# A selective-scan layer on one core: input products made two units ahead in three buffers, state sums taken every two units

## The chip, the core and the metric

The program runs on one core of a Trainium2 chip. The metric is the device time of one execution in microseconds (us); a kernel's time is the median of several executions. The engines are named as in the profile: PE multiplies matrices, PEld loads its weights, DVE is the vector engine, ACT the scalar engine, POOL the general one (GpSimd), SP issues most transfers. Each engine takes its instructions in the order in which the program lists them, and waits at one whose inputs or buffers aren't ready.

## What is computed

Four sequences of 512 steps and 512 channels pass through three residual blocks, each after a layer norm. The change touches the first block, a selective scan over 1024 inner channels with 16 states each:

```python
def step(h, inputs):
    d_t, B_t, C_t, u_t = inputs
    dA = jnp.exp(d_t[..., None] * A)
    h = h * dA + (d_t * u_t)[..., None] * B_t[:, None, :]
    y = jnp.einsum('bdn,bn->bd', h, C_t)
    return (h, y)
...
y = jnp.swapaxes(ys, 0, 1) + u * D
y = y * jax.nn.silu(jnp.transpose(z, (0, 2, 1)))
```

Here `u` is a convolved and gated projection of the input, and `d_t` a softplus of another one. The second block is a pair of linear layers with quantized operands. The third is a mixture of 16 experts, two for each token, with one shared expert.

## The kernel before

**Units of the scan.** The scan goes through the four sequences (batches, b = 0 to 3) one after another, and through each in eight chunks c of 128 channels. A chunk has eight units n; a unit holds 64 channels and 4 of the 16 states, as a tile of 128 partitions by 2 x 512 steps. `UNITS` gives for each n the state group g and the half p of the chunk's channels: p = 0 for n = 0, 1, 4, 5 and p = 1 for n = 2, 3, 6, 7. There are 4 x 8 x 8 = 256 units, here numbered 0 to 255. One turn of the loop in `scan_batch` is called a slot, and slot n scans unit n.

**What a unit costs.** Two exponentials on ACT write the decays `da` (L663; two buffers, in PSUM). One product on POOL writes the inputs `bu` = B x (step x u) (L665; two buffers). On DVE the scan runs over `da` and `bu` and writes into `da` (L672), and a product with C writes `h` (L678; five buffers). PE sums `h` over states into one accumulator `py` (L690), after a product that adds u x D (L686). When all eight units are summed, DVE gates the result into `u` (`gated`, L712).

**When they are issued.** Slot n issues `unit_inputs` of unit n + 1 (decays and product), later the scan of unit n and its product with C. The sums come twice for each chunk: those of units 0 to 3 at slot 4, those of units 4 to 7 at slot 0 of the next chunk, and the gating at slot 1.

**What the products read.** `delta` computes the steps of a chunk: PE (L610), six passes on ACT (L622 to L632), and four on POOL (L634 to L640) with a small fill (L642) that ends them. `spread` then copies the result, with SP, into `rep` (L650; three buffers, one for each half-chunk, 2 x 512 KB), in which each row stands four times. B and C come in `bc` tiles (L601), loaded anew for each batch by `scan_bc`.

**Work beside the scan.** While the scan runs, the kernel computes the inputs of later batches (`front`: projections on PE, ACT's convolution taps L447 and L452, POOL's additions L456) and finishes earlier ones (`back`: output projection, quantized layers, routing; `experts`: tiles of 128 tokens, each with two gathers issued by POOL, L1419 and L1175). These are generators that yield what they wait for. `Pace` estimates, while the program is built, how far each engine has got. `more` is called three times in a slot and issues the next step of each generator if `Pace.clear` allows it: no engine of the step may be more than `BEHIND` (ns) behind the estimate of DVE's time, and what the step waits for must be ready at most `SLACK` (ns) after it; engines other than DVE get an allowance of 3500, 1200 or 0 ns on top, by the place in the slot. For POOL they are 500 and -300. Where steps of a chunk are late for their copy, `end` issues them at once. So the order of instructions on each engine is fixed when the program is built.

After the last scan, the rest of batch 3 (output projection, quantized layers, routing) and the remaining expert tiles run; two gathers for each 128 tokens and DVE's L1223 write the output.

Of the kernel before, what the change touches and what calls it, by code (L numbers as in the profile page):

```python
# [19 lines left out]
P = 128  # L20
# [112 lines left out]
class Pace:  # L133
# [6 lines left out]
    TABLES = {"Exp": 0, "Tanh": 0, "Silu": 1, "Ln": 2}  # L140


    SLACK = {"DVE": 200, "Activation": 700, "Pool": -300, "PE": 3500, "SP": 500}
    BEHIND = {"DVE": 0, "Activation": 1500, "Pool": 500, "PE": 5000, "SP": 4000}

    def __init__(self, nc):
        self.nc, self.seen, self.table, self.queue = nc, 0, None, 0
# [122 lines left out]
class Kernel:  # L270
# [225 lines left out]
    def first_front(self, sb, bank):  # L496

        nc, st = self.nc, self.state[0]
        xnT = self.xnT0
        for j in range(4):  # L500
            self.load_win(0, sb, j)
        for _ in self.layernormed(0, sb, bank, xnT):
            pass
        nc.sync.dma_start(self.wx_sb, self.wx)
        nc.sync.dma_start(self.wdt_sb, self.wdt)
        pj = {}
        pdt = bank.take([P, L])
        pbc = bank.take([P, L])


        pairs = [(b, self.fsideT[b], 0, k) for b in range(B) for k in (0, 2)]
        pairs += [(b, self.ctxwT[b], NK, 0) for b in range(B)]
        each = -(-len(pairs) // NC)
        held = {}

        def columns(c):
            for i in range(c * each, min((c + 1) * each, len(pairs))):
                b, w, _, k = pairs[i]
                held[i] = self.sb.tile([P, NP, L], F32, name="h", bufs=5)
# [36 lines left out]
        st["dt"] = self.sb.tile([P, L], F32, name="dt", bufs=1)  # L556
        nc.scalar.copy(st["dt"], pdt)
        bank.done(pdt)
        rows = sb.tile([2 * DS, L], F32, name="rows", bufs=1)
        nc.scalar.copy(rows, pbc[: 2 * DS])  # L560
        bank.done(pbc)
        nc.sync.dma_start(self.rows_d[0], rows)
        self.done.add(("rows", 0))
        for g in range(NG):
            self.scan_bc(0, g)
# [86 lines left out]
            )  # L652
        st["rep"][c, p] = rep

    def unit_inputs(self, b, c, n):

        nc, st = self.nc, self.state[b]
        g, p = UNITS[n]
        rep = st["rep"][c, p]
        da = self.pscan.tile([P, NP, L], F32, name="da", bufs=2)  # L660
        for i in range(NP):
            q = c * NQC + p * NP + i
            nc.scalar.activation(da[:, i, :], rep[:, i, 0, :], AF.Exp, scale=self.a_sb[:, q, g : g + 1])  # L663
        bu = self.sb.tile([P, NP, L], F32, name="bu", bufs=2)
        nc.gpsimd.tensor_mul(bu, st["bc"][0, g].unsqueeze(1).to_broadcast([P, NP, L]), rep[:, :, 1, :])  # L665
        st["da"][c, n], st["bu"][c, n] = da, bu

    def unit_scan(self, b, c, n):
        st = self.state[b]
# [4 lines left out]
    def unit_out(self, b, c, n):  # L674
        st = self.state[b]
        g, p = UNITS[n]
        h = self.sb.tile([P, NP, L], F32, name="h", bufs=5)
        self.nc.vector.tensor_mul(h, st["da"].pop((c, n)), st["bc"][1, g].unsqueeze(1).to_broadcast([P, NP, L]))  # L678
        st["h"][c, g, p] = h

    def state_sums(self, b, c, g0):

        nc, st = self.nc, self.state[b]
        if g0 == 0:
            st["py"] = self.pscan.tile([P, L], F32, name="py", bufs=1)
            nc.tensor.matmul(st["py"], self.skips.pop((b, c)), st["u"][c], start=True, stop=False)  # L686
        py = st["py"]
        for g in range(g0, g0 + 2):
            for q in range(NQC):
                nc.tensor.matmul(  # L690
                    py[q * CH : (q + 1) * CH, :],
                    self.sel,
                    st["h"][c, g, q // NP][:, q % NP, :],
                    start=False,
                    stop=(g == NG - 1),
                )

    def skip(self, b, c):
# [798 lines left out]
    def run(self, ctx):  # L1497
# [21 lines left out]
        with tc.tile_pool(name="front", bufs=2) as fsb:  # L1519
# [16 lines left out]
            self.unit_inputs(0, 0, 0)  # L1536
# [61 lines left out]
    def finish(self, b, n):  # L1598

        if n == 0:  # L1600
            self.state_sums(b, NC - 1, NG // 2)
        elif n == 1:
            self.gated(b, NC - 1)

    def scan_batch(self, b, beside):

        self.started.add(b)
        for i in range(NC * NU):
# [3 lines left out]

            nb, nc = following(b, c, (n + 1) // NU)
            if nb < B:
                self.unit_inputs(nb, nc, (n + 1) % NU)

            if n == 4:
                self.state_sums(b, c, 0)
            if n == 0 and c:
                self.state_sums(b, c - 1, NG // 2)  # L1620
            if b and not c:
                self.finish(b - 1, n)
            self.more(beside, 3500)
# [5 lines left out]
            if n == 2:  # L1629
                self.gate(b, c)  # L1630
                self.steps_of(*following(b, c, 2))

            if n == 5:
                self.skip(*following(b, c, 2))
                self.copies.append((*following(b, c, 1), 1))
            if n == 7:
                self.copies.append((*following(b, c, 2), 0))
            while self.copies:
                db, dc, p = self.copies[0]
                if db < B:  # L1640
# [78 lines left out]
```

## Time and profile before

| what | us |
|---|---|
| median of three runs (1672.4 to 1674.71) | 1673.51 |
| the profiled execution | 1669.61 |
| its span | 1667.9 |
| first scan starts | 89.7 |
| last scan ends | 1343.9 |
| DVE busy from first to last scan, 1254.2 us | 1076.2 |
| POOL busy in the same | 974.5 |
| PE busy in the same | 926.4 |
| ACT busy in the same | 779.1 |

The profile is one execution. A group line names the source line, engine, operation, tiles (written <- read) and count, then the busy time and the mean of one in ns, then the idle time of the engine just before such instructions and what ended most of it. A line of the waits names who waited for whom, the total in us, the number of times and the longest. A line of the timeline has the start, the duration, the instruction, and in brackets the idle time before it and what ended it. [...]

### The profile page before, as it was taken

How to read it: one execution, taken by the hardware profiler on the slowest of the kernel's cores; microseconds unless marked ns; L12 is line 12 of the kernel's file. 1: busy time of each engine (PE TensorE's matmuls, PEld its weight loads, DVE VectorE, ACT ScalarE, POOL GpSimd, SP SyncE). 2: the span in 40 equal slices, each digit the busy share in tenths (PEclk: the TensorE clock that was granted, in tenths of full speed). 3: DMA queues.
4: the chain of work that ended last, by engine and by line, in shares of the span. 5: the costliest groups of instructions: out<-in, count | busy, mean ns of one | idle time of the engine just before them, and what ended most of it. 6: DMA issues, size and time to landing. Idle time of an engine off the chain costs nothing. (4 is left out here: it accounts for less than half of the span.)

```text
span 1667.9 us, 15571 instructions
## 1 busy us (share of the span) xinstructions
PE 1216.4 (73%) x4552; PEld 585.6 (35%) x4552; DVE 1220.5 (73%) x1322; ACT 895.6 (54%) x1448; POOL 1125.6 (67%) x904
## 2 busy tenths in 40 slices
PE   6867588649676759799776985875656897668980
PEld 2222122103242323233433432363434346434760
DVE  4377899998898896789887998988777933453312
ACT  2365677654668764654886652478654313530330
POOL 1176999887788894777887874878887544027454
PEclk9988789768787978799988897987797999768995
DMA  5564464565463463675443758535577472158957
GB/s 204 150 160 111 98 148 95 125 150 148 106 123 67 110 167 107 152 194 155 91 106 88 194 126 292 139 105 146 146 212 207 123 299 105 52 204 295 360 207 221
DMA packets 109657, 262.21 MB, mean 157 GB/s; under 512 B 16192, under 2 KB 20416, under 8 KB 109504
## 3 DMA queue, kind: packets, MB, share of 16 engines
q1 hardware_dynamic: 93120, 204.50, 46.7%
q0 software_dynamic: 16448, 56.65, 9.8%
q8 instruction: 40, 0.66, 0.2%
q14 instruction: 49, 0.40, 0.1%
HBM read 168.55 MB, written 45.88 MB: 129 GB/s over the span
## 5 line engine op out<-in xcount | busy, mean ns | idle before, releaser
L665 POOL TENSOR_TENSOR bu<-bc,rep 128x1024 f32<-128x1024 f32 x256 | 602.0, 2357 | 171.2 <-DVE da L672 130.5
L672 DVE TENSOR_TENSOR_SCAN da<-da,bu 128x1024 f32<-128x1024 f32 x256 | 585.8, 2288 | 81.2 <-POOL bu L665 60.3
L663 ACT ACTIVATE da<-rep,a_sb 128x512 f32<-128x512 f32 x512 | 352.9, 691 | 298.8 <-DVE h L678 261.5
L678 DVE TENSOR_TENSOR h<-da,bc 128x1024 f32<-128x1024 f32 x256 | 312.0, 1219 | 15.6 <-PE py L690 5.1
L690 PE MATMUL py<-h,sel 128*32 128x512 f32 x1024 | 172.2, 673 | 68.5 <-DVE h L678 68.4
L1175 POOL DMA_INDIRECT wx<-in_wexp,wrow x62 | 62.9, 1015 | 92.6 <-PE bank L1465 29.0
L400 PE MATMUL bank_a<-xnT,win 128*128 128x512 f32 x176 | 91.2, 666 | 12.9 <-DVE gz L357 8.3
L456 POOL TENSOR_TENSOR u<-u,tap 128x511 f32<-128x511 f32 (+2 forms) x72 | 91.2, 1266 | 9.2 <-ACT tap L452 6.7
L690 PEld LDWEIGHTS py<-h,sel 128*32 128x32 f32 x1024 | 30.6, 116 | 187.3 <-DVE h L678 109.9
L400 PE MATMUL bank_g<-xnT,win 128*128 128x512 f32 x176 | 90.0, 659 | 4.4 <-DVE gz L357 2.1
L1419 POOL DMA_INDIRECT xs<-xn_d,tok x62 | 64.0, 1032 | 19.7 <-issue 15.2
L400 PE MATMUL bank_b<-xnT,win 128*128 128x512 f32 x128 | 64.0, 646 | 17.1 <-ACT sp_r L623 17.1
L400 PEld LDWEIGHTS bank_a<-xnT,win 128*128 128x128 f32 x176 | 36.5, 215 | 62.8 <-issue 48.1
L634 POOL TENSOR_TENSOR sp_e<-sp_e,dd 128x512 f32<-128x512 f32 x32 | 40.6, 1270 | 26.2 <-ACT dd L629 26.0
L400 PEld LDWEIGHTS bank_g<-xnT,win 128*128 128x128 f32 x176 | 36.3, 214 | 59.3 <-issue 48.8
L335 POOL TENSOR_SCALAR ln_scale<-ln_mv 128x1 f32<-128x1 f32 x48 | 11.0, 229 | 61.6 <-DVE ln_mv L328 58.5
L686 PE MATMUL py<-u,skip 128*128 128x512 f32 x64 | 37.5, 671 | 13.5 <-DVE u L712 13.5
L1213 POOL DMA_INDIRECT yg<-y_d,pos x32 | 32.5, 1014 | 21.3 <-DMA y_d<-ys 9.3
L400 PEld LDWEIGHTS bank_b<-xnT,win 128*128 128x128 f32 x128 | 26.4, 212 | 52.9 <-issue 29.4
L1223 DVE SCALAR_TENSOR_TENSOR xr<-yg,topw,xr 128x512 f32<-128x512 f32 x32 | 23.8, 751 | 28.4 <-DMA yg<-y_d,pos 27.8
L640 POOL TENSOR_TENSOR dd<-dd,u 128x512 f32<-128x512 f32 x32 | 40.6, 1269 | 1.5
L636 POOL TENSOR_TENSOR sp_e<-sp_e,sp_r 128x512 f32<-128x512 f32 x32 | 40.6, 1268 | 1.4
(404 smaller groups left out, 2386.4 us busy)
## 6 DMA issues: line engine op xcount, KB each, us to landing
rep<-dd SPq DMA_DIRECT2D x128, 512.0 KB
win<-in_win SPq DMA_DIRECT2D x64, 256.0 KB
x<-xr SPq DMA_DIRECT2D x48, 256.0 KB
xr<-x SPq DMA_DIRECT2D x48, 256.0 KB
y_d<-ys SPq DMA_DIRECT2D x48, 256.0 KB
bc<-rows_d SPq DMA_DIRECT2D x32, 256.0 KB
gz_d<-gz SPq DMA_DIRECT2D x32, 256.0 KB
gzl<-gz_d SPq DMA_DIRECT2D x32, 256.0 KB
```

The lines of the kernel that those rows point to most:

```text
L400: nc.tensor.matmul(pj, win[:, k, :], xnT[:, k, :], start=(k == 0), stop=(k == NK - 1))
L456: nc.gpsimd.tensor_add(u[:, j:], u[:, j:], v[j][:, j:])
L634: nc.gpsimd.tensor_sub(e, e, du)
L636: nc.gpsimd.tensor_add(e, e, r)
L640: nc.gpsimd.tensor_mul(du, delta, st["u"][c])
L663: nc.scalar.activation(da[:, i, :], rep[:, i, 0, :], AF.Exp, scale=self.a_sb[:, q, g : g + 1])
L665: nc.gpsimd.tensor_mul(bu, st["bc"][0, g].unsqueeze(1).to_broadcast([P, NP, L]), rep[:, :, 1, :])
L672: self.nc.vector.tensor_tensor_scan(daf, daf, buf, 0.0, ALU.mult, ALU.add)
L678: self.nc.vector.tensor_mul(h, st["da"].pop((c, n)), st["bc"][1, g].unsqueeze(1).to_broadcast([P, NP, L]))
L690: nc.tensor.matmul(py[q * CH : (q + 1) * CH, :], self.sel, st["h"][c, g, q // NP][:, q % NP, :], start=False, stop=(g == NG - 1),)
L1175: nc.gpsimd.indirect_dma_start(out=ws[s], out_offset=None, in_=self.wexp, in_offset=bass.IndirectOffsetOnAxis(ap=wrow[:, s : s + 1], axis= ...
L1419: nc.gpsimd.indirect_dma_start(out=xs[s], out_offset=None, in_=xn_d, in_offset=bass.IndirectOffsetOnAxis(ap=tok[:, s : s + 1], axis=0), bo ...
```

## The change

`unit_inputs` is split. The decays stay one unit ahead. The products are issued two units ahead, into three buffers, at the same place of the slot; the first two are issued before the loop. `h` gives up one of its five buffers for the third `bu`. The state sums are taken for each two units: units n - 2 and n - 1 at slot 2, 4 and 6, the last two at slot 0 of the next chunk. The copies of the steps are queued and forced one slot earlier, the second half's at slot 4, the next chunk's first half at slot 6. B and C of the next batch, first half, are loaded at slot 3, not 4. `Pace` lets POOL be 3500 ns behind, not 500, and lets its steps wait 2500 ns, not -300.

```diff
-    SLACK = {"DVE": 200, "Activation": 700, "Pool": -300, "PE": 3500, "SP": 500}
-    BEHIND = {"DVE": 0, "Activation": 1500, "Pool": 500, "PE": 5000, "SP": 4000}
+    SLACK = {"DVE": 200, "Activation": 700, "Pool": 2500, "PE": 3500, "SP": 500}
+    BEHIND = {"DVE": 0, "Activation": 1500, "Pool": 3500, "PE": 5000, "SP": 4000}
...
-        bu = self.sb.tile([P, NP, L], F32, name="bu", bufs=2)
-        nc.gpsimd.tensor_mul(bu, st["bc"][0, g].unsqueeze(1).to_broadcast([P, NP, L]), rep[:, :, 1, :])
-        st["da"][c, n], st["bu"][c, n] = da, bu
+        st["da"][c, n] = da
+
+    def unit_products(self, b, c, n):
...
+        bu = self.sb.tile([P, NP, L], F32, name="bu", bufs=3)
+        nc.gpsimd.tensor_mul(
+            bu, st["bc"][0, g].unsqueeze(1).to_broadcast([P, NP, L]), st["rep"][c, p][:, :, 1, :]
+        )
+        st["bu"][c, n] = bu
...
-        h = self.sb.tile([P, NP, L], F32, name="h", bufs=5)
+        h = self.sb.tile([P, NP, L], F32, name="h", bufs=4)
...
-        for g in range(g0, g0 + 2):
-            for q in range(NQC):
+        for g, p in UNITS[2 * i : 2 * i + 2]:
+            h = st["h"].pop((c, g, p))
+            for j in range(NP):
+                q = p * NP + j
...
             nb, nc = following(b, c, (n + 1) // NU)
             if nb < B:
-                self.unit_inputs(nb, nc, (n + 1) % NU)
-
-            if n == 4:
-                self.state_sums(b, c, 0)
+                self.unit_decays(nb, nc, (n + 1) % NU)
+            nb, nc = following(b, c, (n + 2) // NU)
+            if nb < B:
+                self.unit_products(nb, nc, (n + 2) % NU)
+
+            if n and n % 2 == 0:
+                self.state_sums(b, c, n // 2 - 1)
             if n == 0 and c:
-                self.state_sums(b, c - 1, NG // 2)
+                self.state_sums(b, c - 1, NU // 2 - 1)
...
+            if n == 4:
+                self.copies.append((*following(b, c, 1), 1))
             if n == 5:
                 self.skip(*following(b, c, 2))
-                self.copies.append((*following(b, c, 1), 1))
-            if n == 7:
+            if n == 6:
                 self.copies.append((*following(b, c, 2), 0))
...
-                    late = (db, dc) == following(b, c, 1) and n == NU - 2 + p or (db, dc) == (b, c)
+                    late = (db, dc) == following(b, c, 1) and n == NU - 3 + p or (db, dc) == (b, c)
...
-            if b + 1 < B and c == NC - 1 and n in (4, 7):
+            if b + 1 < B and c == NC - 1 and n in (3, 7):
```

More of the change, by code (lines that the diff above doesn't have):

```diff
@@ L518, in columns @@
                 b, w, _, k = pairs[i]
-                held[i] = self.sb.tile([P, NP, L], F32, name="h", bufs=5)
+                held[i] = self.sb.tile([P, NP, L], F32, name="h", bufs=4)
                 nc.sync.dma_start(held[i], w[k * P : (k + 2) * P, :].rearrange("(k p) n -> p k n", k=2))
@@ L653, in spread, with unit_decays @@
         st["rep"][c, p] = rep
-    def unit_inputs(self, b, c, n):
+    def unit_decays(self, b, c, n):
         nc, st = self.nc, self.state[b]
@@ L663, in unit_inputs @@
             nc.scalar.activation(da[:, i, :], rep[:, i, 0, :], AF.Exp, scale=self.a_sb[:, q, g : g + 1])
-        bu = self.sb.tile([P, NP, L], F32, name="bu", bufs=2)
-        nc.gpsimd.tensor_mul(bu, st["bc"][0, g].unsqueeze(1).to_broadcast([P, NP, L]), rep[:, :, 1, :])
-        st["da"][c, n], st["bu"][c, n] = da, bu
+        st["da"][c, n] = da
+    def unit_products(self, b, c, n):
+        nc, st = self.nc, self.state[b]
+        g, p = UNITS[n]
+        bu = self.sb.tile([P, NP, L], F32, name="bu", bufs=3)
[3 more added lines that the diff above has]
+        st["bu"][c, n] = bu
     def unit_scan(self, b, c, n):
@@ L676, in unit_out, with state_sums @@
         g, p = UNITS[n]
-        h = self.sb.tile([P, NP, L], F32, name="h", bufs=5)
+        h = self.sb.tile([P, NP, L], F32, name="h", bufs=4)
         self.nc.vector.tensor_mul(h, st["da"].pop((c, n)), st["bc"][1, g].unsqueeze(1).to_broadcast([P, NP, L]))
         st["h"][c, g, p] = h
-    def state_sums(self, b, c, g0):
+    def state_sums(self, b, c, i):
         nc, st = self.nc, self.state[b]
-        if g0 == 0:
+        if i == 0:
             st["py"] = self.pscan.tile([P, L], F32, name="py", bufs=1)
@@ L687, in state_sums @@
         py = st["py"]
-        for g in range(g0, g0 + 2):
-            for q in range(NQC):
+        for g, p in UNITS[2 * i : 2 * i + 2]:
+            h = st["h"].pop((c, g, p))
+            for j in range(NP):
+                q = p * NP + j
                 nc.tensor.matmul(
[L691 to L695, printed above, removed]
+                    py[q * CH : (q + 1) * CH, :], self.sel, h[:, j, :], start=False, stop=(g == NG - 1)
                 )
@@ L1535, in run @@
             self.fronts = Steps(self.pace, (w for b in range(1, B) for w in self.front(b)))
-            self.unit_inputs(0, 0, 0)
+            self.unit_decays(0, 0, 0)
+            for n in range(2):
+                self.unit_products(0, 0, n)
             pool = ctx.enter_context(ExitStack())
@@ L1600, in finish @@
         if n == 0:
-            self.state_sums(b, NC - 1, NG // 2)
+            self.state_sums(b, NC - 1, NU // 2 - 1)
         elif n == 1:
```

## The prediction

> **What bounds the kernel now.** I read the busy time by stages first, cut at the first scan's start and the last scan's end. Columns: busy time and count of PE, PEld, DVE, ACT, POOL, then the granted clock and the share of the transfer engines.
>
> ```profile
> 89.70:1343.90 1254.20, 926.43 (x3280) 409.46 (x3281) 1076.22 (x1007) 779.09 (x1225) 974.48 (x718) 0.85 0.55 139
> 1343.90:1667.90 324.00, 230.72 (x1141) 153.27 (x1139) 108.78 (x269) 86.35 (x181) 137.75 (x156) 0.84 0.63 222
> ```
>
> The chain of waits that ended last covers only the final 36 us, so the stages decide. The scan stage is three quarters of the span, and DVE is its fullest engine, 1076.2 of 1254.2 us. Nothing shortens that work, so the change can win at most DVE's idle time there, 178 us. POOL has 974.5, 86% to 78%. Next, the groups of a unit on the page:
>
> ```profile
> L665 POOL TENSOR_TENSOR bu<-bc,rep 128x1024 f32<-128x1024 f32 x256 | 602.0, 2357 | 171.2 <-DVE da L672 130.5
> L672 DVE TENSOR_TENSOR_SCAN da<-da,bu 128x1024 f32<-128x1024 f32 x256 | 585.8, 2288 | 81.2 <-POOL bu L665 60.3
> L663 ACT ACTIVATE da<-rep,a_sb 128x512 f32<-128x512 f32 x512 | 352.9, 691 | 298.8 <-DVE h L678 261.5
> L678 DVE TENSOR_TENSOR h<-da,bc 128x1024 f32<-128x1024 f32 x256 | 312.0, 1219 | 15.6 <-PE py L690 5.1
> ```
>
> A unit is 2.288 + 1.219 = 3.51 us of DVE. POOL needs 2.357 for its product, and waits 130.5 us for scans to give back a `bu` buffer while DVE waits 60.3 us for products: two engines that stop each other in turn. What DVE waited for in the stage (window from 89 us on):
>
> ```profile
> DVE da L672 <- POOL bu L665: 60.3, 22, 27.4
> DVE da L672 <- ACT da L663: 20.6, 17, 5.7
> DVE u L712 <- PE py L690: 15.8, 5, 7.6
> ...
> DVE h L678 <- PE py L690: 5.1, 3, 2.6
> ```
>
> The longest, 27.42 us, stands before the first scan. That leaves 21 waits for products in the stage, 60.3 - 27.42 = 32.9 us. DVE's timeline shows three long ones, 8.58 (at 169.77), 4.10 (1251.61) and 5.17 us (1267.99), together 17.85; the other 18 lie between 0.15 and 1.67 us and make 15.0. A short one, POOL's lines and then DVE's:
>
> ```profile
> 203.32 1.26 POOL L638 TENSOR_TENSOR dd<-sp_e,sp_w 128x512 f32<-128x512 f32 x1
> 204.55 2.35 POOL L665 TENSOR_TENSOR bu<-bc,rep 128x1024 f32<-128x1024 f32 x1
> ```
>
> ```profile
> 206.93 2.30 DVE L672 TENSOR_TENSOR_SCAN da<-da,bu 128x1024 f32<-128x1024 f32 x1 [1.24 <-POOL bu L665]
> ```
>
> Two steps of 1.26 us (L636, L638) stood in POOL's queue ahead of a product that DVE needed at once. The long one at 169.77:
>
> ```profile
> 156.90 1.27 POOL L640 TENSOR_TENSOR dd<-dd,u 128x512 f32<-128x512 f32 x1
> 158.24 0.10 POOL L642 MEMSET dd<- 128x1 f32 x1
> 167.39 4.66 POOL L665 TENSOR_TENSOR bu<-bc,rep 128x1024 f32<-128x1024 f32 x2 [9.06 <-DMA rep<-dd]
> ```
>
> Here the steps of chunk (0, 2) were ready only at 158.3, and their copy took 9.06 us; that at 1267.99 is the same at chunk (3, 6) (6.69 us of POOL's idle time before it).
>
> **Products two ahead.** In slot n the product goes out at the same place as before, and it waits for the same event: before, product n + 1 with two buffers, now product n + 2 with three, both for scan n - 1. So POOL gets no more work and no later start; each product is only due a unit later, 3.51 us at least. Against this, `Pace` lets POOL's other steps run 3.0 us further behind (500 to 3500), so up to 3.0 of the 3.51 can be filled with queued steps, and behind a step that waits stand the products, for which DVE waits.
> - Short waits, 15.0 us. At best all go. If the planner fills all it may, each loses 0.51 us: five are 0.49 or less, 1.48 together, and 13 lose 0.51, 8.1 in all. In the built order the largest heaps of other steps between two products are hardly larger than before, so I take 12.
> - Long waits, 17.85. Each can lose 3.51: 3 x 3.51 = 10.5. They lose nothing if the copy is what comes last; the decays need it too, and stay one ahead. In the built order the end of the steps (L642) stands at the same product as before in both chunks, so one slot earlier. I take 6.
> - What is late next is the decays: 0.691 x 2 = 1.4 us of ACT after the last read of their buffer, beside a scan of 2.29, so 0.9 us to spare. In nearly all the short waits longer than 0.3 us the decays had ended 1.8 us or more before DVE came free: at 206.93 ACT's pair ended at 203.52, and DVE at 205.69. Some waits will pass to them: I set 4 us against the gain (bounds 0 and 10; their waits are 20.6 now).
>
> **State sums by two units.** The same 512 matrix products. Sixteen records took 1.92 us at 533.96; after a chunk's last `h` half as many are left before gating, 0.96 us less in each of the five waits of L712 (15.8 us) and in the one after the last scan (3.12): 5 us. An `h` buffer is now asked back four units after it was written, its sums issued two slots earlier, about 9 us (2 x 3.51 + 2.29) ahead of need, where it was 5.8 (3.51 + 2.29): the 5.1 us of L678 should go. Against it PE now stops for an `h` four times a chunk, not twice; it stopped 109.9 + 68.4 us (PEld and PE, overlapping) without being the fullest engine, but what stands behind it on PE (projections for ACT and POOL) starts later. Between +10 and -5 I take 6.
>
> **Copies and loads a slot earlier.** The same 128 copies and 32 loads of B and C on SP's queue, with their 512 and 256 KB, in nearly the same order; SP's wait for the last reader of `rep` (38.7 us for ACT, 13.9 for POOL) is off DVE's path. I count nothing. If a copy is late after all, it costs what the row at 167.39 shows, up to 9 us a time. The second half of B and C isn't loaded earlier, though needed a slot earlier; no wait for `bc` stands in the trace, so nothing.
>
> **After the last scan.** In the built order 48 expert tiles are left, not 46. From 1549.94 to 1628.84 the second group's 23 weight gathers go out, 3.6 us a tile, so two tiles cost 7 us uncovered. They are of the first group and lie ahead of batch 3's routing, which is bound by its chain of layers: from 1400 to 1480 PE is busy 54.6 of 80 us. But from 1344 to 1380 PE is busy 35.7 of 36 us. Bounds 0 and 7; I take 2.
>
> **A rule that speaks against it.** All products ran 2336 to 2697 ns, median 2355, beside scans of 2264 to 2299: neither shows that it had to wait for the other. The Trainium skill, "SBUF — State Buffer", "Who interferes with whom", says that a DVE instruction with two SBUF inputs and a GpSimd one that reads SBUF exclude each other. Scan and product with C each read one operand from PSUM, and the trace agrees. If the rule caught them, a unit would be 2.29 + 1.22 + 2.36 = 5.9 us, and lead would be worth nothing; units took 4.9 us on average, background work included.
>
> **The sum.** 12 + 6 - 4 + 6 - 2 = 18 us. The profiled execution took 1669.61 (span 1667.9 and 1.7 around it), 3.9 below the median of 1673.51; I take the same difference off the median: 1655.5.
>
> **Rivals.**
> - The lead is spent by the planner, and the decays take over the waits: 8 from the short waits, nothing from the long, 2 from PE, less 2 and 2: -6, 1667.5. For it: the thresholds return 3.0 of 3.51 us. Against it: a queue that is filled only at times still gains.
> - The stage gains and the end gives it back: 7 us for the tiles, and PE's stops taking the 5 that they may, 18 - 5 - 11 = 2: 1671.5, no change. For it: PE and transfers (0.94) are full at 1344 to 1380. Against it: the slack until 1480.
> - Slower: POOL waits at the head of its queue. Its steps may now be queued 2.5 us before their inputs are ready, where 0.3 us after was asked, 2.8 in all. In the first batch POOL is already nearly as full as DVE (230.2 and 241.2 of 270.4 us; 96.9 of 100 from 200 to 300), so a wait of 2.8 us in each of its eight chunks, 22 us, is paid there. With half of the gains left (12 of 18 with the rest): 1673.5 + 22 - 12 = 1683.5. It decides from the point at which such waits in a slot exceed the 3.51 us of lead. For it: the steps wait for ACT now already (L634 for L629 16.1 us in 7). Against it: in the built order the other steps stand in nearly the same slots.
>
> **How the numbers follow.** Forecast 0.52, planner 0.18, end 0.10, slower 0.20. The range goes from all bounds on the good side, 15 + 10.5 + 10 = 35.5 less, 1638, to the slow rival, 1684. About 0.2%, 3.3 us, is what a measurement can tell from no change: faster 0.68 (forecast, and nearly all of the planner's case), same 0.12, slower 0.20.
>
> **What would show it.** Right: DVE's waits for products in the stage fall from 32.9 to some 15 us, three long ones among them; POOL's wait for scans stays near 130; the waits of L712 and L678 for PE fall by half; DVE's busy time in the stage stays at 1076. Wrong: waits for the decays well above 25 us, POOL's waits at L634 or L456 for ACT doubled, or an end longer than 331 us after the last scan. My range fails if batch 3's tiles or the order of the quantized layers move so that DVE waits for PE or POOL in new places, which the counts can't tell.

## The result, and the profile after

| | kernel before | changed kernel |
|---|---|---|
| median of 20 runs each, us | 1670.90 | 1673.28 |
| the profiled execution, us (its span) | 1669.61 (1667.9) | 1679.47 (1677.7) |
| first scan to last scan, us | 1254.2 | 1265.8 |
| after the last scan, us | 324.0 | 320.4 |

The ratio of the times is 1.0009, 95% interval 0.9996 to 1.0022: no change that can be told. (A ratio here is taken over all runs and can differ by some 0.001 from that of the two medians.) The forecast was 1655.5. The profiled execution of the changed kernel is 6 us above its median; what only its length shows is not used below.

The groups of the changed kernel that answer to those shown of before, with one more, the sums on PE:

```profile
L671 POOL TENSOR_TENSOR bu<-bc,rep 128x1024 f32<-128x1024 f32 x256 | 601.4, 2360 | 172.9 <-DVE da L680 117.7
L680 DVE TENSOR_TENSOR_SCAN da<-da,bu 128x1024 f32<-128x1024 f32 x256 | 585.8, 2288 | 81.5 <-POOL bu L671 48.0
L663 ACT ACTIVATE da<-rep,a_sb 128x512 f32<-128x512 f32 x512 | 352.9, 691 | 253.2 <-DVE h L686 221.2
L700 PE MATMUL py<-h,sel 128*32 128x512 f32 x1024 | 279.0, 676 | 82.1 <-DVE h L686 81.9
L686 DVE TENSOR_TENSOR h<-da,bc 128x1024 f32<-128x1024 f32 x256 | 312.0, 1219 | 12.8 <-PE py L700 1.8
```

Its waits of DVE over the whole span (who waited for whom, total in us, times, longest):

```profile
DVE da L680 <- POOL bu L671: 48.0, 7, 27.2
DVE da L680 <- ACT da L663: 31.5, 23, 5.2
...
DVE xn L1081 <- PE bank_a L1058: 16.3, 4, 9.7
...
DVE xr L1096 <- PE bank_g L1090: 10.8, 5, 2.7
...
DVE u L718 <- PE py L700: 9.8, 6, 3.6
```

The stage and the rest (us, busy us of PE, PEld, DVE, ACT, POOL, with instructions, then PE's granted clock, the transfers' share, GB/s):

```profile
91.50:1357.30 1265.80, 1002.82 (x3270) 411.84 (x3270) 1073.62 (x1005) 775.00 (x1222) 971.01 (x712) 0.88 0.55 137
1357.30:1677.70 320.40, 230.15 (x1150) 155.25 (x1150) 108.86 (x271) 86.87 (x184) 143.13 (x163) 0.84 0.64 228
```

Three things are to be seen. What the change aims at came: without the wait of 27.2 before the first scan, DVE waits 20.8 us for products in the stage, 32.9 before, and less for the sums. Other waits grew: decays from 20.6 to 31.5, and DVE in front of the shared expert's results (L1081 16.6 and L1096 21.2 us in the stage; the same lines took 6.3 and 7.5 before). And DVE's own work in the stage is the same (1073.6 and 1076.2), while PE is busy 76 us longer there (1002.8 and 926.4). A second profile of the same instructions (s2 below, span 1667.1 us) has the same two waits: 20.9 us for products, 30.6 for decays.

### The profile page after: what moved, and what is told of

Its sections match the earlier page's. It is cut to its first block, busy times and chain, and to the rows that moved or that the text cites. A ratio compares the mean times of both kernels' runs of the same rounds, so it can differ in the third digit from the quotient of the medians.

```text
span 1677.7 us, 15580 instructions
## 1 busy us (share of the span) xinstructions
PE 1294.1 (77%) x4552; PEld 590.7 (35%) x4552; DVE 1218.2 (73%) x1322; ACT 892.2 (53%) x1448; POOL 1127.5 (67%) x904
## 5 line engine op out<-in xcount | busy, mean ns | idle before, releaser
L671 POOL TENSOR_TENSOR bu<-bc,rep 128x1024 f32<-128x1024 f32 x256 | 601.4, 2360 | 172.9 <-DVE da L680 117.7
L700 PE MATMUL py<-h,sel 128*32 128x512 f32 x1024 | 279.0, 676 | 82.1 <-DVE h L686 81.9
L700 PEld LDWEIGHTS py<-h,sel 128*32 128x32 f32 x1024 | 47.7, 116 | 264.0 <-DVE h L686 134.0
L1181 POOL DMA_INDIRECT wx<-in_wexp,wrow x62 | 63.0, 1016 | 93.4 <-PE bank_g L1471 24.7
L456 POOL TENSOR_TENSOR u<-u,tap 128x511 f32<-128x511 f32 (+2 forms) x72 | 91.2, 1267 | 38.0 <-ACT tap L452 35.7
L400 PE MATMUL bank_g<-xnT,win 128*128 128x512 f32 x216 | 109.3, 653 | 0.8 <-ACT xnT L386 0.7
L400 PE MATMUL bank_a<-xnT,win 128*128 128x512 f32 x144 | 69.8, 630 | 2.2 <-DVE gz L357 1.2
L400 PEld LDWEIGHTS bank_g<-xnT,win 128*128 128x128 f32 x216 | 43.4, 209 | 62.2 <-issue 56.0
L694 PE MATMUL py<-u,skip 128*128 128x512 f32 x64 | 37.1, 664 | 24.7 <-DVE u L718 24.7
L357 DVE SCALAR_TENSOR_TENSOR hs<-hs,bank 128x128 f32<-128x128 f32 x24 | 6.9, 286 | 53.3 <-ACT hs L1462 40.7
L341 ACT ACTIVATE xn<-xr,ln_scale 128x512 f32<-128x512 f32 x32 | 25.6, 808 | 37.2 <-POOL ln_scale L337 37.2
L1456 PE MATMUL bank<-xT,wx 128*128 128x128 f32 x368 | 44.3, 277 | 0.0
```

The lines of the kernel that those rows point to most:

```text
L400: nc.tensor.matmul(pj, win[:, k, :], xnT[:, k, :], start=(k == 0), stop=(k == NK - 1))
L456: nc.gpsimd.tensor_add(u[:, j:], u[:, j:], v[j][:, j:])
L700: nc.tensor.matmul(py[q * CH : (q + 1) * CH, :], self.sel, h[:, j, :], start=False, stop=(g == NG - 1))
L1181: nc.gpsimd.indirect_dma_start(out=ws[s], out_offset=None, in_=self.wexp, in_offset=bass.IndirectOffsetOnAxis(ap=wrow[:, s : s + 1], axis= ...
L1456: nc.tensor.matmul(ph[:, i, :], w[:, o : o + P], xT[:, k, :], start=(k == 0), stop=(k == NK - 1))
```

## The experiments

**Theories.** (1) The lead is worth 12 to 25 us, and another placement of background steps, above all near the last scans, gives it back. (2) The lead gains nothing. (3) The sums for each two units cost what the lead gains. Two more came up later: (4) a placement of background steps fits only the loop that it was planned for, and loop and placement have no price apart; (5) the sums hold PE longer.

Loop and placement move together, since the planner (`Pace`) places the steps of each loop anew. To part them, its choices were written down for one kernel (the steps that each call of `more` issues, the slot of each copy, the choice of expert tiles) and replayed in another. The core of that edit, here with P for the recorded choices:

```diff
-            x.go_if_clear(x.due(self.slot) if x.due else 0)
+            at = 2 * self.turn + (x.name in seen)
+            seen.add(x.name)
+            if not x.over and x.written < P["steps"][x.name].get(at, 0):
+                x.go()
```

"Old placement" is that of the kernel before, "new placement" that of the changed kernel. All replayed kernels but e4, e12 and e14 have the changed kernel's copies and loads of B and C, s1 too; on the old placement three of the 62 copies came one unit earlier by that than recorded. That a replay costs nothing by itself is seen in e12, where the old loop, but for the order of its sums, runs on its own recorded placement: 0.9997. Each time is a ratio to the kernel before on the same chip, since chips differ (the kernel before took 1657 to 1673 us).

| loop | placement | ratio (95% interval) |
|---|---|---|
| before | old (its own) | 1 |
| + sums by two (e4) | old | 1.0177 (1.0146 to 1.0209) |
| + sums by two, four h (e9) | old | 1.0184 (1.0154 to 1.0214) |
| + sums by two, four h, lead (e1) | old | 1.0172 (1.0144 to 1.0201) |
| + lead, four h, sums by four (e3) | old | 1.0261 (1.0233 to 1.0289) |
| before, with the copies and loads of the change (s1) | new | 1.0063 (1.0041 to 1.0085) |
| + sums by two, four h (e2) | new | 1.0052 (1.0033 to 1.0071) |
| + sums by two, four h, lead: the changed kernel | new (its own) | 1.0009 (0.9996 to 1.0022) |

### The new loop on the old placement, and its lead taken away

The first kernel is the changed one with the old placement replayed (the edit above and nothing else).

> The changed loop (products two units ahead, three buffers for bu, four for h, sums over states for each two units), but every background step, copy and expert tile written at the opportunity at which the kernel before wrote it. Theory 1 (the lead is worth 12 to 25 us in the scan stage, and the other placement of background steps gives it back near the last scans): 1648 to 1660 us, 11 to 22 below the kernel before. Theory 2 (the lead gains nothing: DVE's waits for products become waits for decays and POOL's for taps): 1668 to 1674, like the kernel before. Theory 3 (the lead gains, the sums for each two units cost it back): 1668 to 1676 too, told from theory 2 by e3. In the trace theory 1 wants DVE's waits for bu at about 20 us instead of 33 and the last scan 10 to 20 us earlier than 1343.9.

It took 1688.51 us (kernel before 1658.98), ratio 1.0172: slower, against all three theories. The waits for products fell (45.8 us with the 27.3 before the first scan), yet the last scan ended at 1377.4.

In the second the lead alone is undone, on the new placement:

```diff
-            for n in range(2):
+            for n in range(1):
                 self.unit_products(0, 0, n)
...
-            nb, nc = following(b, c, (n + 2) // NU)
+            nb, nc = following(b, c, (n + 1) // NU)
             if nb < B:
-                self.unit_products(nb, nc, (n + 2) % NU)
+                self.unit_products(nb, nc, (n + 1) % NU)
...
-name="bu", bufs=3
+name="bu", bufs=2
```

> The changed kernel with one thing undone, the lead: products one unit ahead and two buffers for bu; sums, buffers of h and the placement of all background steps stay those of the changed kernel. Theory 1: 8 to 20 us slower than the changed kernel (1673.3), so 1681 to 1694, with DVE's waits for bu back at 30 us or more. Theory 2: 1669 to 1677, the same as the changed kernel. Theory 3: 1681 to 1694, as theory 1.

1667.38 against 1658.98, ratio 1.0052; the changed kernel's was 1.0009. So the lead is worth 0.43%, some 7 us, here, a little less than theories 1 and 3 had (8 to 20). Its waits of DVE:

```profile
DVE da L683 <- POOL bu L674: 97.0, 39, 27.5
DVE da L683 <- ACT da L666: 15.5, 11, 4.7
```

With the lead those for products are 49.0 less (97.0 to 48.0), and those for decays 16.0 more (15.5 to 31.5). Added up over the stage, DVE's idle time went only from 199.0 to 192.1 us. One place shows how. Here is POOL, one unit ahead, and then DVE at unit 169 (start, duration, instruction; in brackets the idle time before it and what ended it):

```profile
874.31 1.26 POOL L952 TENSOR_TENSOR w<-w,rwsc_row 128x512 f32<-128x512 f32 x1
881.25 1.27 POOL L459 TENSOR_TENSOR u<-u,tap 128x511 f32<-128x511 f32 x1 [5.68 <-ACT tap L455]
882.47 1.26 POOL L952 TENSOR_TENSOR w<-w,rwsc_row 128x512 f32<-128x512 f32 x1
883.70 1.27 POOL L459 TENSOR_TENSOR u<-u,tap 128x510 f32<-128x510 f32 x1
884.94 2.35 POOL L674 TENSOR_TENSOR bu<-bc,rep 128x1024 f32<-128x1024 f32 x1
```

```profile
887.32 2.30 DVE L683 TENSOR_TENSOR_SCAN da<-da,bu 128x1024 f32<-128x1024 f32 x1 [5.04 <-POOL bu L674]
```

POOL stood 5.68 us for a tap, with two more steps and then the product behind it; that is the rival of the prediction that has POOL wait at the head of its queue. In the changed kernel the product of this unit ended 8.43 us before DVE was free. But ACT, which had stood for a projection and then worked off what had come late, wrote the decays only now:

```profile
871.68 0.69 ACT L447 ACTIVATE u<-bank_g,convw_sb 128x512 f32<-128x512 f32 x1 [2.50 <-PE bank_g L400]
872.26 1.83 ACT L452 ACTIVATE tap<-bank_g,convw_sb 128x511 f32<-128x511 f32 x3
873.97 0.73 ACT L977 ACTIVATE xq<-xn 128x256 bf16<-128x256 f32 x2
874.58 0.73 ACT L953 ACTIVATE w<-w,s 128x512 f32<-128x512 f32 x1
875.20 1.43 ACT L663 ACTIVATE da<-rep,a_sb 128x512 f32<-128x512 f32 x2
```

```profile
876.72 2.30 DVE L680 TENSOR_TENSOR_SCAN da<-da,bu 128x1024 f32<-128x1024 f32 x1 [2.19 <-ACT da L663]
```

So 5.04 became 2.19, not nothing: with one unit of lead the decays had been 2.58 us late there too, behind the product. On the old placement e9 and e1 (below) differ in the lead in the same way: waits for products 57.8 to 45.8, for decays 26.8 to 31.8, ratio 1.0184 and 1.0172.

### What five h, sums by four and the last 16 units are worth

With the lead, three `bu` and the sums by four of before, on the old placement, with four buffers of `h`:

```diff
-            if n and n % 2 == 0:
-                self.state_sums(b, c, n // 2 - 1)
+            if n == 4:
+                self.state_sums(b, c, 0)
```

> The lead alone: products two units ahead and three buffers for bu, the sums over states in two halves of a chunk as before, on the placement of the kernel before; h has four buffers, since five and three do not fit together. Theory 1: 1650 to 1666, some of e1's gain (DVE may wait for a buffer of h). Theory 2: 1668 to 1676. Theory 3: 1645 to 1656, faster than e1 by 5 us or more.

1701.30, ratio 1.0261, the slowest but one, and slower than any theory had it. `DVE h L689` waited 74.5 us (26 times) for PE's sums, 5.1 before. So the sums by two are what makes the third buffer of `bu` payable: they free `h` two units earlier.

In the next run (e7), the changed kernel keeps its placement up to unit 240 and then has the old one.

> The changed kernel with its own placement up to unit 240, and from there on (the last 16 units of the scan, and the order of the steps behind it) the placement of the kernel before. Theory 1, in the form that the last chunk alone gives the gain back (it took 55.8 us against 36.1): 1650 to 1662, 11 to 23 below the changed kernel. If the gain is lost elsewhere or was never there (theory 2): 1668 to 1676.

1685.11, ratio 1.0152, slower than either expectation. Its scan stage took 1248.3 us and the rest 343.2. On the same chip e2, which keeps the new placement to its end and lacks the lead, had 1273.5 and 300.7. So the stage is 25 us shorter (some 7 of them by the lead) and the rest 42 longer: what is taken from in front of the last scans has to run behind them, here in an order that was not made for it. Theory 1's "the last chunk alone" fell.

### The sums by two

The kernel before on its own placement, with only the sums changed as the change does it:

```diff
-            if n == 4:
-                self.state_sums(b, c, 0)
+            if n and n % 2 == 0:
+                self.state_sums(b, c, n // 2 - 1)
```

> The kernel before, on its own placement, with the sums over states made for each two units instead of each four, and nothing else changed (products one ahead, two buffers of bu, five of h). Theory 3, now narrowed (the new order of the sums costs: TensorE stands for DVE's multiply of the gate and for h twice as often, in front of matmuls that DVE waits for): 8 to 25 us slower than the kernel before, most of e1's 28.5 us. Theory 4 (the loop as such costs nothing; a placement of background steps fits only the loop that it was planned for): within 5 us of the kernel before.

1687.20 against 1656.82, ratio 1.0177: all of e1's loss. The group of the sums in the kernel before, then in this one:

```profile
L690 PE MATMUL py<-h,sel 128*32 128x512 f32 x1024 | 172.2, 673 | 68.5 <-DVE h L678 68.4
```

```profile
L695 PE MATMUL py<-h,sel 128*32 128x512 f32 x1024 | 282.5, 679 | 65.3 <-DVE h L681 65.1
```

The same 1024 records, two for each of the 512 products and each as long as before (673 and 679 ns), take 110 us more of PE. The timeline tells why; first a half-chunk of the kernel before, then two units of e4:

```profile
386.00 1.92 PE L690 MATMUL py<-h,sel 128*32 128x512 f32 x16
```

```profile
385.25 1.91 PE L695 MATMUL py<-h,sel 128*32 128x512 f32 x8
```

Eight records take as long as sixteen. Each product writes one of four bands of 32 rows of `py`. In the kernel before, the records of four bands start 7 ns apart and run side by side. Two units of the same half of a chunk (same p) have two bands, so only two run at a time. The Trainium skill, "TensorE: Matmul & The Clock Gate", "Part 3: Packing small matmuls — row/col tiling", has matmuls of 32 output columns run at once in distinct column groups, three of them 2.38 times as fast; the two rows above are such a case, with four and with two.

In e4 ACT's waits for PE in the stage rose from 121.5 to 184.1 us (added up over the trace), DVE's waits for decays from 20.6 to 32.2, while its waits at the gating and for `h` fell by 10.5 in the stage (15.8 + 5.1 to 10.3 + 0.1). A path of the loss that fits is PE late, ACT's steps late, the decays behind them late. It is argued, not shown, and not all: DVE idled 25.7 us more in the stage (178.0 and 203.7), and the decays are 11.6 of them.

The same with the changed kernel's four `h`, one unit ahead (e2's diff on the old placement):

> e1 without the lead: sums for each two units and four buffers of h, products one ahead in two buffers, on the placement of the kernel before. If the lead is worth the 7 us that e2 showed on the other placement, too: 5 to 10 us slower than e1, so 1.020 to 1.024 of the kernel before. If the lead itself is what costs on this placement: 1.000 to 1.010 of the kernel before. Beside e4 it also shows what the fifth buffer of h is worth: 0 to 5 us by every theory.

1687.07, ratio 1.0184, between the two expectations. The fifth `h` is worth nothing once the sums come by two, and the lead makes no difference that can be told here (1.0184 and 1.0172).

Is it PE's time, or PE's stops? First the order of the products in each half-chunk was changed in the kernel before, so that two bands alternate:

```diff
-        for g in range(g0, g0 + 2):
-            for q in range(NQC):
+        for p in range(NQC // NP):
+            for g, q in [(g, p * NP + j) for g in range(g0, g0 + 2) for j in range(NP)]:
```

> The kernel before on its own placement, with only the order of the eight matmuls in each half of the sums changed: those of the first two units ahead of those of the last two, so that two bands of 32 rows of py alternate where four took turns. Same stops for h, same buffers, same lead. Theory 5 (width: matmuls of different bands run side by side, four with four bands and two with two, so the sums hold TensorE longer, and what waits behind them is late): TensorE's busy time for the sums from 172 to about 280 us, and 12 to 30 us slower than the kernel before (1.007 to 1.018). Theory 3 in its old form (stops: what costs is that TensorE stands for h and for the gate more often): within 3 us of the kernel before.

Ratio 0.9997 (0.9972 to 1.0022), but PE's busy time for the sums was 179.6 us, not 280: the records still start in fours, two pairs 20 ns apart, so four still ran at a time. The run didn't do what it was made for and decides nothing between the theories; it only shows that with this order, all eight products in one go, PE loses little.

Then the pairs of e4 were shifted by one unit, so that most have four bands:

```diff
-            if n == 4:
-                self.state_sums(b, c, 0)
+            if n > 1 and n % 2:
+                self.state_sums(b, c, [0, 1, 2] if n == 3 else [n - 2, n - 1])
```

> e4 with the pairs shifted by one unit: sums of units 0, 1 and 2 at unit 3, of 3 and 4 at unit 5, of 5 and 6 at unit 7, of 7 at the next chunk's first. TensorE stops as often as in e4, but the two units of most pairs belong to different copies, so four bands take turns. Theory 5: TensorE's busy time for the sums 200 to 225 us, and 0 to 10 us slower than the kernel before (1.000 to 1.006). Stops: as e4, 1.012 to 1.018.

PE's time for the sums fell nearly as expected, to 228.7 us, and the time did not: 1.0204 (1.0174 to 1.0234). Theory 5 fell for the old placement: half of PE's extra time was taken off and nothing came back. "Stops" had it lower, too (1.018 at most); the shifted pairs also stand a unit later, which this run doesn't tell from their width.

> e1 (lead, three buffers of bu, four of h, placement of the kernel before) with the shifted pairs of e14. Theory 5, with a lead worth 2 to 13 us: 0.992 to 1.004 of the kernel before. Stops: 1.012 to 1.017, as e1.

The same shift with the lead, on the old placement: 1.0289 (1.0257 to 1.0321), slower than both expectations.

### The planner left free

Two kernels in which the planner places the steps itself. The first is the kernel before with POOL's two figures alone:

```diff
-    SLACK = {"DVE": 200, "Activation": 700, "Pool": -300, "PE": 3500, "SP": 500}
-    BEHIND = {"DVE": 0, "Activation": 1500, "Pool": 500, "PE": 5000, "SP": 4000}
+    SLACK = {"DVE": 200, "Activation": 700, "Pool": 2500, "PE": 3500, "SP": 500}
+    BEHIND = {"DVE": 0, "Activation": 1500, "Pool": 3500, "PE": 5000, "SP": 4000}
```

> The kernel before with the two new figures for POOL in the planner's table alone (slack 2500 for -300, behind 3500 for 500); the planner then places the background steps anew. Theory 3: 0 to 10 us slower or faster, by the placement. Theory 4: the same range; what it adds is how far a new placement alone moves the time, and whether the stage's waits for products (33 us) grow when POOL is let run behind, to 45 us or more.

0.9981 (0.9963 to 0.9999). The waits for products grew by 24 us (60.3 to 84.3 with the first), and others fell by as much: DVE idled 177.0 us in the stage, 178.0 before. So the new figures by themselves cost the old loop nothing.

> The changed kernel with products one ahead in two buffers, as in e2, but with the background steps placed by the planner for this loop. If e2's 7 us over the changed kernel are the lead's own worth: 1.003 to 1.007 of the kernel before. If a placement made for another loop costs by itself (theory 4): faster than e2, 0.996 to 1.003.

1.0089 (1.0055 to 1.0123), above both expectations and not faster than e2 with the same loop: the planner's own placement needn't be better than one made for another loop, so theory 4 doesn't hold in its strict form.

Next the shifted pairs in the changed kernel:

> The changed kernel with the shifted pairs, all else as it is, the planner placing the background steps for this loop. Theory 5: 0.985 to 0.997 of the kernel before, that is 6 to 26 us below the changed kernel. Stops: 0.998 to 1.004, as the changed kernel.

1636.19 against 1673.07, ratio 0.9767 (0.9737 to 0.9797): faster than both kernels and than theory 5 had it, with the loop that took 1.0289 on the old placement. One loop, two placements, 5.3% apart.

### One figure of the planner

To see how far a placement moves the time by chance, DVE's slack was moved by a quarter in three kernels:

```diff
-    SLACK = {"DVE": 200,
+    SLACK = {"DVE": 150,
```

> e13 (the changed kernel with shifted pairs, 0.977 of the kernel before) with the planner's slack for DVE at 150 instead of 200: the same loop and computation, another placement. If the shift's gain belongs to the loop: 0.970 to 0.985. If it is the chance of one placement: anywhere from 0.985 to 1.01.

> The changed kernel (1.001 of the kernel before) with the planner's slack for DVE at 150 instead of 200. If the time belongs to the loop: 0.996 to 1.006. If placements move it by chance: outside of that, by 0.5 to 2 per cent.

> The kernel before with the planner's slack for DVE at 150 instead of 200. If the time belongs to the loop: 0.996 to 1.006. If placements move it by chance: outside of that, by 0.5 to 2 per cent.

p1: 0.9835 (0.9809 to 0.9862). p2: 0.9844 (0.9816 to 0.9871), that is 1632.34 against 1658.50. p3: 1.0019 (1.0001 to 1.0037). So p1 is still in the range set for a gain that belongs to the loop, p3 in that for a time that belongs to the loop, and p2 outside of the latter: the changed loop itself, untouched, is 1.6% faster on a neighbouring placement, and there the shifted pairs are worth nothing that can be told (0.9835 and 0.9844). In p2, too, the sums take PE 282.5 us, and the waits of DVE are:

```profile
DVE da L680 <- ACT da L663: 34.8, 26, 4.9
DVE da L680 <- POOL bu L671: 32.7, 5, 27.2
```

Decays wait as long as in the changed kernel; products cost 5.5 us after the first scan where it was 20.8. One difference is plain. In the changed kernel POOL ends the steps of chunk (0, 2) at 157.2, and the product in front of unit 16 waits for their copy:

```profile
157.11 0.10 POOL L642 MEMSET dd<- 128x1 f32 x1
166.88 4.65 POOL L671 TENSOR_TENSOR bu<-bc,rep 128x1024 f32<-128x1024 f32 x2 [9.67 <-DMA rep<-dd]
```

In p2 those steps are placed 11 us earlier:

```profile
146.05 0.10 POOL L642 MEMSET dd<- 128x1 f32 x1
...
156.67 2.35 POOL L671 TENSOR_TENSOR bu<-bc,rep 128x1024 f32<-128x1024 f32 x1 [1.99 <-DMA rep<-dd]
```

DVE's wait there, 8.58 us before and 9.31 in the changed kernel, is gone in p2, and unit 16 is scanned at 159.6 instead of 169.3. The second long wait for a product, at unit 240, is 3.2 us there and 7.3 in the changed kernel.

In the changed kernel the first pair's sums were then written one unit later, to take PE's stop for the gate away:

```diff
-            if n and n % 2 == 0:
+            if n in (3, 4, 6):
                 self.state_sums(b, c, n // 2 - 1)
```

> The changed kernel with the sums of a chunk's first pair written one unit later (at unit 3 instead of 2), the other pairs where they were; the pairs keep two bands, so TensorE's time for the sums stays near 279 us. If the loss of the sums is the stop for the gate at a chunk's start: that wait from 25 us to under 8, and 0.98 to 0.993 of the kernel before. If it is TensorE's longer time for two bands: 0.996 to 1.006. The chance of a placement, as p1 to p3 show it, is the error of both.

1.0120 (1.0089 to 1.0150), outside both expectations; that wait fell only from 24.7 to 18.9 us, while it was 8.6 in p2, where the pairs stand as in the change. It follows the placement, and the run decides nothing.

### The old loop on the new placement

The mirror of e4: e2 with the sums by four and five `h`. It keeps the changed kernel's copies and loads.

> The loop of the kernel before (products one ahead, two buffers of bu, five of h, sums by four) on the placement of the changed kernel: e2 with the sums by four. If the sums for each two units cost what e4 showed wherever they stand: 0.985 to 0.995 of the kernel before, so 1 to 2 per cent below e2 (1.005). If e4's loss is that of a loop on a placement made for another: 1.005 to 1.025, at or above e2.

1683.92 against 1672.64, ratio 1.0063 (1.0041 to 1.0085). The sums take PE 172.3 us here and 280.9 in e2, yet e2 is no slower (1.0052). So the 1.8% of e4 are not a price of the sums that holds wherever they stand; they belong to these sums on that placement.

The whole of PE grew less than the sums did. The stage in s1, then in e2 (columns as above):

```profile
89.70:1364.50 1274.80, 933.69 (x3270) 412.44 (x3270) 1073.99 (x1005) 775.97 (x1222) 971.94 (x711) 0.83 0.54 136
```

```profile
88.80:1362.20 1273.40, 997.98 (x3270) 408.56 (x3270) 1074.41 (x1005) 774.76 (x1222) 971.16 (x711) 0.88 0.55 136
```

The sums are 108.6 us longer and all of PE 64.3, so its other work took 44 us less; the 216 records of the projections into `bank_g` (L403) took 684 ns on average in s1 and 639 in e2. The granted clock of the runs goes with that: 0.832 to 0.841 in s1 and 0.876 to 0.884 in e2, and over all kernels here 0.832 to 0.856 with sums by four and 0.865 to 0.889 with pairs of two bands. No run holds the clock, so it stays open what the longer sums would cost at an equal one.

> The changed kernel with the planner's slack for DVE at 250 instead of 200 (150 gave 0.984 of the kernel before, 200 gave 1.001). If the changed loop is the faster one and its own placement was an unlucky one: 0.98 to 0.992. If 150 was the lucky one: 0.996 to 1.012.

The third placement was none: at a slack of 250 the planner made the same choices, and the program is the changed kernel's, instruction for instruction. 0.9997 (0.9975 to 1.0019) repeats 1.0009. It ran on the same chip as s1, 1672.56 beside 1683.92 us: on this placement the changed loop is the faster one by 0.7%.

## Why the prediction failed

**What the zero is made of.** On the new placement, step by step: the old loop costs 0.63% more than on its own; sums by two and four `h` change nothing that can be told (1.0063 to 1.0052); the lead gives 0.43% (1.0052 to 1.0009). In us of 1671: +10.5, -2, -7. The sum had 20 us for the loop (12 + 6 - 4 + 6) and set 2 against them for the steps that move. Of the 20 about 9 came, and against them stood 10.5. (These are the placement together with the earlier copies and loads, which s1 has too; e4 and e9 differ in those and were alike, 1.0177 and 1.0184.)

**The step that failed first: two more tiles, 2 us.** That was all the sum held for background steps that move; measured in its place, s1 against the kernel before, are 10.5 us. It left every other wait of DVE where the profile of before had it. The planner placed the steps anew, and DVE met new waits. In s1 DVE's waits for products in the stage are 72.1 us, 32.9 before, with POOL's waits for taps at 40.1, 6.7 before. Near the last scans the shared expert came in front of them; PE and then DVE in the changed kernel:

```profile
1305.41 6.03 PE L1066 MATMUL bank_b<-xnT,ws 128*128 128x512 f32 x8 [7.60 <-DMA ws<-in_wexp]
1311.28 3.60 PE L1058 MATMUL bank_a<-xnT,ws 128*128 128x512 f32 x8
```

```profile
1314.91 0.69 DVE L1081 SCALAR_TENSOR_TENSOR xn<-xn,bank_a 128x512 f32<-128x512 f32 x1 [9.75 <-PE bank_a L1058]
```

PE stood 7.60 us for weights, and DVE 9.75 for PE, with the last chunk's other seven scans behind it. The old loop on the new placement has the same wait:

```profile
1323.67 0.69 DVE L1086 SCALAR_TENSOR_TENSOR xn<-xn,bank_a 128x512 f32<-128x512 f32 x1 [9.63 <-PE bank_a L1063]
```

The last chunk took 55.8 us in the changed kernel, 54.0 and 55.9 in s1 and e2, but 36.2, 35.4 and 35.5 in the kernel before, e4 and e1: it goes with the placement, not with the loop. It is not all lost, though, since that work no longer runs behind the last scan: e7, which took it out of the stage, had a longer end. The prediction named this (new places where DVE waits for PE, "which the counts can't tell") as what would break its range, and gave it no term. It would not have been right with one of this size alone: the same loop on p2's placement was at 1645, 0.9844 of 1671, below the forecast.

**Products two ahead.** Right in what it frees: 32.9 to 20.8 us, and 69.5 to 20.8 against e2. Short waits: 15.0 to 4.2 us, nearly as forecast (12 gained). Long ones, where 6 of 17.85 were to go: 16.6 are left. The wait of 4.10 is gone, but that in front of unit 16 did not lose 3.51 us, it grew from 8.58 to 9.31, and that in front of unit 240 from 5.17 to 7.28, since the copy is what comes last, the bound of "nothing" that the prediction gave. The steps of unit 16 end at the same product as before, but in time that is 157.2, not a slot ahead of 158.3. Those of unit 240 end at 1246.0, 10.6 us earlier than before, and their copies still go out only at 1251.4, since SP's queue holds three stores ahead of them; two of these waited 12.2 us for ACT:

```profile
1237.48 13.33 SPq L810 DMA_DIRECT2D xn_d<-xn  x3
1250.90 0.38 SPq L708 DMA_DIRECT2D skip<-in_skipw  x1
1251.38 7.76 SPq L650 DMA_DIRECT2D rep<-dd  x4
```

Wrong in what is late next: 4 us for decays, bounds 0 and 10, against 11 between the two kernels and 16.0 between e2 and the changed kernel. The reason given, that the decays had ended 1.8 us before DVE came free, held for the short waits of one placement. On the new one POOL runs further behind, and under a long wait for a product lay late decays that came to light, as at unit 169.

**The sums by two, -6.** "Half as many are left before gating, 0.96 us less" is wrong: eight records take 1.91 us where sixteen took 1.92. The waits fell all the same, at the gating from 15.8 to 8.7 and for `h` from 5.1 to 1.8 us in the stage, so the 10 us hoped for came in the rows named. But not by the sums alone: the old sums on the new placement (s1) waited 7.2 us at the gating, and 6.0 for `h`. Measured between s1 and e2, for 6 us in the sum: 0.1%, within the intervals. What takes the rest back is not shown; PE's sums are 107 us longer (172.2 to 279.0), and it stops more often.

**Copies and loads, nothing.** POOL's waits for copies in front of products were not nothing: 43.6 us in the changed kernel (36.3 before), with the copies of unit 240 above as the plainest case. A wait of 7.6 us for a load of B and C, where before had none, was 0.2 in the second profile of the same instructions (s2). What of it reached DVE is in the waits for products above. POOL's wait for scans fell from 130.5 to 117.7 us where the prediction had it near 130, and DVE's busy time stayed.

**The rivals.** "The stage gains and the end gives it back" has the right time, 1671.5, and the wrong place: the end after the last scan was 3.6 us shorter, and the loss stood in front of it. "POOL waits at the head of its queue" was true of the new placement, where POOL's wait for taps (L456 for ACT) went from 6.7 to 35.7 us, one of the prediction's own signs of being wrong, but it was paid with one unit of lead (s1 at 1.0063, products 99.5 us with the first) and mostly covered with two. That is what the lead is for here: it pays back most of what this placement costs. The planner's new figures need not cost anything (e6, 0.9981 with the old loop). "The lead is spent by the planner, and the decays take over the waits" came nearest in kind; it had 6 us of gain, and none came.

**What stays open.** Whether the forecast would hold on a usual placement. The old loop on the three placements that the planner made for it was at 1, 0.9981 and 1.0019, the changed loop on its two at 1.0009 and 0.9844, and with shifted pairs at 0.9767 and 0.9835. So the zero may be bad luck of one placement, as 0.9844 may be good luck of another; two are too few to tell. Why the shifted pairs gave 0.977 and 0.984 on two placements is not shown: on the old placement they were slower than the pairs as they are, and the changed loop reached 0.984 without them. Nor is it shown which of a placement's many waits makes most of the 1.6% between the changed kernel and p2; chunk (0, 2) and the last chunk are two that were seen, about 10 and 5 us.

## What to carry to other kernels

Where a planner or scheduler places work by estimates, an edit has two effects, that of the loop and that of the new placement, and the second can be the larger: here 0.5% and 0.6%, and 1.6% for one figure moved by a quarter. Replay the old placement under the new code and the new one under the old before either is given a price, and try some neighbouring placements before an edit is called worthless. A longer lead on one of two inputs is worth only the distance to the other input, and to what both are made from.

## What was not expected of the hardware

Products with 32 output rows ran four at a time when their bands differed (16 records in 1.92 us) and two at a time when a stop left only two bands (8 records in 1.91 us). Order within a run of eight products hardly mattered: with two bands alternating in the program, records still started in fours, two pairs 20 ns apart, and PE's time was 179.6 us against 172.2. But 109 us more for the sums did not show in the time (s1 and e2). All of PE grew by only 64 us in that stage, its other work taking 44 us less at a granted clock of 0.88 where it was 0.83; that the longer sums raise the clock is not shown by itself.
